# Three more softmax row sums taken off ScalarE in every odd step of an attention block: one to VectorE, two begun on GpSimd and ended on VectorE

## The chip, the cores and the metric

The kernel runs on one core of one Trainium2 chip, as one program. The metric is the device time of one execution in microseconds, taken as the median of several runs. The engines have short names in the views of the profile: PE is TensorE (PEld its weight loads), ACT is ScalarE, DVE is VectorE, POOL is GpSimd, SP is SyncE, which here only issues DMAs.

## What is computed

An attention layer with a condition added to queries and keys, and a residual. `x` is 8 x 512 x 512 in float32, there are 16 heads of 32 columns, and the softmax is over 512 keys.

```python
Q = heads(x @ Wq.T + bq);  K = heads(x @ Wk.T + bk);  V = heads(x @ Wv.T + bv)
cQ = Q + heads(cond @ Wq.T + bq);  cK = K + heads(cond @ Wk.T + bk)
scores = einsum('bhqd,bhkd->bhqk', cQ, cK) / sqrt(32)
x + einsum('bhqk,bhkd->bhqd', softmax(scores), V)      # heads joined again
```

## The kernel before

**Steps and items.** A step `t` is one batch and one group of four heads, so there are 32 steps (8 batches, 4 groups). The loop over `t` from 1 to 28 does each step in four items, `i` = 0 to 3. Item 0 is called `V` in the code: the weighted sum of the step before (`weighted`). The other three make a quarter of the projections for the batch to come, `q`, `k`, `v` in odd steps and `k`, `q`, `v` in even ones, by a Strassen-like scheme with seven products (`four_products` and `three_products`).

**Two ways to the softmax.** Both need the row sums of the exponentials, the softmax's denominators, for 4 query chunks `qc` (128 rows each) and 4 heads `j`: 16 sums a step, called (`qc`, `j`) here and in the code.

- For an even step the scores are made once to find the row maxima and sums (`row_max`, `denominators`), with the exponentials thrown away in PSUM, and a second time transposed (`exponentials`), which gives the operand of the weighted sum.
- For an odd step (`BLOCKED`, `t` = 1, 3 to 27) the exponentials of the first pass are kept in SBUF (the tile `arena`), and DMAs and VectorE's 32 x 32 transposes turn them (`exchange`, `turn_blocks`).

An item looks ahead: at step `t`, items 0 to 2 do maxima and exponentials of chunks 1 to 3 of step `t + 1`, and item 3 does chunk 0 of step `t + 2`. So an odd step's chunk 0 is worked on in item 3 of the odd step before it, and its chunks 1 to 3 in items 0 to 2 of the even step before it.

**Where the sums are made.** `denominators` issues one ScalarE `Exp` for each (`qc`, `j`). With `accum_out` the activation also gives the row sum, and the profile shows it as a second short instruction, ACTIVATION_READ_ACCUMULATOR. For some sums of odd steps from 3 on, `accum_out` is left out and VectorE adds up the exponentials in `arena` (`sum_by_vector`, L729); the table `BY_VECTOR` says which, by the item of the even step that does it:

```python
BY_VECTOR = {1:[(2,0),(2,1)],2:[(3,0),(3,1)]}
```

**Order.** Nothing is scheduled by a tool: each engine runs its instructions in the order in which the code is written, with semaphores between the engines. Names and lines that the steps below use:

- PE: scores L670 (even steps) and L662 (odd steps), transposed scores L784, weighted sum L806, spreading of the sums L843, projections L471.
- ScalarE: `Exp` of the first pass L718, of the second L795, copies of the `v` products out of PSUM L537 and L542.
- VectorE: maxima L626 and L679, reciprocals of the sums L853, the turning of the weighted sum L873, projections' ends L576 and L577, x turned L378, kept exponentials turned L690.
- GpSimd: adds of the projections L559, L561, L563 and L578, of the residual L874 and L875, products for `combine_x` L395 and L396 (in one even step of two), the sums masked L833, a quarter of the exchange's DMAs L701.

PSUM is eight banks; `begin` and `released` give each item its banks in the order in which the items before have let go of them, so a bank that ScalarE or VectorE empties late holds up the matmul that writes it next.

Of the kernel before, what the change touches and what calls it, by code (L numbers as in the profile page):

```python
# [12 lines left out]
ALU = mybir.AluOpType  # L13
AX = mybir.AxisListType
# [3 lines left out]
def kernel(  # L18
# [38 lines left out]
    nc = tc.nc  # L57
    P = 128
# [4 lines left out]
    HG = P // HD  # L63
# [8 lines left out]
    EARLY = 3  # L72
    SINGLY = "qk"
    BY_POOL = (3,)
    BY_VECTOR = {1:[(2,0),(2,1)],2:[(3,0),(3,1)]}
    HELPED = "qk"
    WARM = (48, 4)
    BLOCKED = list(range(1, T - 4, 2))
# [45 lines left out]
    def banks(i, n=1):  # L124

        row = row_of[0] or [at_end[j] for j in TURNS[turn[0]]]
        j = row[i]
        if n == 1:
            return psum[:, j, :]
        k = row[i + 1]  # L130
        return psum[:, j : k + 1 : k - j, :]
# [7 lines left out]
    def begin(w):  # L139
        rows = order[w : w + 4]  # L140
        pairs = [(j, j + 1) for j in rows if j + 1 in rows]
        last = max(pairs, key=lambda p: rows.index(p[0]) + rows.index(p[1]), default=sorted(rows[2:]))
        order[w : w + 4] = sorted(j for j in rows if j not in last) + list(last)
        row_of[0] = list(order)

    def released(*roles):
        order[:] = [row_of[0][i] for i in roles]
# [57 lines left out]
    def add_bias(t):  # L205

        if turned_by_vector(t):
            bias = bvs[:, t % G, :].unsqueeze(1).broadcast_to([P, NB, BL])
        else:
            bias = bvl.broadcast_to([P, S])  # L210
        nc.gpsimd.tensor_tensor(xr[t], xr[t], bias, ALU.add)  # L211
# [12 lines left out]
    def rows_kept(t, half):  # L224

        a = arena[:, half * HG : (half + 1) * HG, :]
        return a.rearrange("p g (c h s) -> p g c h s", c=2, h=HG)
# [104 lines left out]
    def in_place(b):  # L332
# [5 lines left out]
    wT = {  # L338
        n: const.tile([P, NC, D], F32, tag=f"wT{n}", name=f"wT_{n}") for n in ("q", "k", "v")
    }  # L340
# [277 lines left out]
    sums = {}  # L618
# [84 lines left out]
    def denominators(t, qc, w=HG, js=range(HG)):  # L703

        if t >= T - 2:
            return
        for j in js:
            if t in BLOCKED:
                to = rows_kept(t, qc // 2)[:, :, qc % 2, j, :].rearrange(
                    "p g (c e) -> p g c e", e=BL  # L710
                )
            else:
                to = banks(w + j)
            of = banks(w + j)
            if t in BLOCKED:
                of = of.rearrange("p (c g e) -> p g c e", g=HG, e=BL)
            by_vector = t in BLOCKED and t > 1 and any((qc, j) in a for a in BY_VECTOR.values())
            nc.scalar.activation(  # L718
                to,
                of,  # L720
                AF.Exp,
                bias=nmax[t][:, qc, j, :],
                **({} if by_vector else {"accum_out": sums[t][:, qc, j, :]}),
            )

    def sum_by_vector(t, qc, j):

        if t in BLOCKED:
            nc.vector.tensor_reduce(  # L729
                sums[t][:, qc, j, :], rows_kept(t, qc // 2)[:, :, qc % 2, j, :], AX.XY, ALU.add  # L730
            )
# [65 lines left out]
    def times_v(t, kc, pt, chunks=range(NS), half=None):  # L797
        b, g = divmod(t, G)
        at = slice(0, S) if half is None else slice(half * HS, (half + 1) * HS)
        cs = slice(0, NS) if half is None else slice(half * 2, half * 2 + 2)  # L800
        for j in range(HG):
            if t in BLOCKED:
                e = blocked[t][:, :, cs, j, kc * BL : (kc + 1) * BL].rearrange("p a c e -> p c a e")
            else:
                e = es[t, kc, j // 2][:, j % 2, at]
            nc.tensor.matmul(  # L806
                pt[j * HD : (j + 1) * HD, at],
                vs[b % 2][:, kc, (g * HG + j) * HD : (g * HG + j + 1) * HD],
                e,
                start=(kc == chunks[0]),  # L810
                stop=(kc == chunks[-1]),
            )
# [13 lines left out]
    def masked(t):  # L826

        if t in aparts:
            return aparts.pop(t)
        apart = wT["k"][:, t % 2, P : P + HG * NS * NS].rearrange(  # L830
            "p (h c a) -> p h c a", h=HG, c=NS
        )
        nc.gpsimd.tensor_tensor(  # L833
            apart,
            sums[t].rearrange("p c h o -> p h c o").broadcast_to([P, HG, NS, NS]),
            which.unsqueeze(1).unsqueeze(1).broadcast_to([P, HG, NS, NS]),
            ALU.mult,
        )
        return apart

    def spread_sums(apart, pd):
        for h in range(HG):
            nc.tensor.matmul(  # L843
                pd[h * BL : (h + 1) * BL, :NB],
                modulo,
                apart[:, h].rearrange("p c a -> p (c a)"),
                start=True,
                stop=True,
            )

    def reciprocals(t, pd):
        rec = op.tile([P, NB, 1], F32, tag="recs", name=f"recs_{t}")
        nc.vector.reciprocal(rec, pd[:, :NB].unsqueeze(2))  # L853
        return rec

    def weighted(t, pt, pd, between):

        if t:
            add_bias(t)
        apart = masked(t)  # L860
        for half in range(2) if t in BLOCKED else (None,):
            for kc in range(NS):
                times_v(t, kc, pt, half=half)
                if kc == 0 and half != 1:
                    spread_sums(apart, pd)
        rec = reciprocals(t, pd)
        between()
        send(t, pt, rec)

    def send(t, y_, rec):  # L870

        y = op.tile([P, NB, BL], F32, tag="res", name=f"res_{t}", bufs=1)
        nc.vector.transpose(y.rearrange("p f e -> p (f e)"), y_)  # L873
        nc.gpsimd.tensor_tensor(y, y, rec.broadcast_to([P, NB, BL]), ALU.mult)  # L874
        nc.gpsimd.tensor_tensor(xr[t], y, xr[t], ALU.add)  # L875
        if t % 2 or t >= T - 4:
            to_store.append(t)
# [284 lines left out]
        (0, 3): [],  # L1162
    }

    for t in range(1, T - 3):
        b, r = divmod(t, G)
        blocks = t in BLOCKED
        w = 0 if blocks else HG
        items = ["V", "q", "k", "v"] if blocks else ["V", "k", "q", "v"]
        for i, item in enumerate(items):  # L1170
            rows = (t + 1, i + 1) if i < 3 else (t + 2, 0)
            begin(w)
            if not blocks:
                exponentials(t, i)
            late_first = item in ("v" if blocks else "qkv") and t % 2 == 1
            hold = row_max(*rows, late_first, w, not blocks and item in SINGLY)

            def held(i=i, hold=hold):
                hold()
                if i == 2:  # L1180
                    split_max(t + 1)
                    turn_max(t + 1)

            dens = lambda js=range(HG): denominators(*rows, w, js)
            if item in "qkv":
                products(t, item, blocks, held, dens, nothing)
            else:
                held()
                dens()
                if blocks:  # L1190
                    weighted(t - 1, banks(4), banks(5), nothing)
                    released(6, 7, 0, 1, 2, 3, 5, 4)
                else:
                    weighted(t - 1, banks(0), banks(1), nothing)
                    released(2, 3, 1, 4, 5, 6, 7, 0)
            if i == 0 and r % 2 == 0:
                turn_x(t + NC + 2)
                turn_x(t + NC + 3)
            if i == 0 and r == 1:
                combine_x(b + 1, 1, nc.gpsimd)  # L1200
            if i == 1 and r == 0:
                combine_x(b + 1, 0, nc.gpsimd)
            if i == 2:
                aparts[t] = masked(t)
            turn_more(t, i)
            if not blocks:
                for qc, j in BY_VECTOR.get(i, ()):
                    sum_by_vector(t + 1, qc, j)
            for what in ORDERS[t % 2, i]:
                if what == "store":  # L1210
                    store()
                elif what == "residual":
                    if 3 < t + 1 <= T - 4:
                        load_residual(t + 1)
                elif what == "x":
                    load_pairs()
                elif t + 1 in BLOCKED:
                    exchange(t + 1, what)
# [67 lines left out]
    t = T - 3  # L1286
# [25 lines left out]
    t = T - 2  # L1312
# [25 lines left out]
    t = T - 1  # L1338
# [61 lines left out]
    b, g = divmod(t, G)  # L1400
# [55 lines left out]
```

## Time and profile before

| what | value |
|---|---|
| median of 3 runs | 658.34 us (658.25 to 658.65) |
| the profiled execution | 658.21 us, of which its span is 656.1 us |
| granted TensorE clock | 0.999 |
| PE matmuls busy | 649.3 us |
| PE weight loads busy | 305.2 us |
| VectorE busy | 596.4 us |
| ScalarE busy | 538.4 us |
| GpSimd busy | 356.5 us |

Busy time is the time in which at least one instruction of the engine ran. Two steps, an odd and an even one, take 38.9 us together and repeat from about 83 us to 590 us. The readings below are from the pair whose even step begins at 316.70 us (items at 316.70, 322.54, 327.31 and 332.22 us).

### The profile page before, as it was taken

The numbers are of one execution on the slowest core, as the hardware profiler recorded it, in microseconds if no ns is written. First come the engines' busy times: TensorE is split into PE (matmuls) and PEld (weight loads), VectorE is DVE, ScalarE is ACT, GpSimd is POOL, SyncE is SP. The second block draws the span as 40 slices with busy tenths as digits, with TensorE's granted clock in tenths as the row PEclk, the third lists the DMA queues.
The fourth block names the chain that finished last, engine by engine and source line by source line (L and its number), as shares of the span: only waits on it lengthen the run. The fifth ranks groups of instructions, "written<-read, shape, count | busy, mean of one in ns | idle before, by whom it ended". The sixth has DMA issues, their size and how long they took to land.

```text
span 656.1 us, 23961 instructions
## 1 busy us (share of the span) xinstructions
PE 649.3 (99%) x9568; PEld 305.2 (47%) x9568; DVE 596.4 (91%) x868; ACT 538.4 (82%) x1341; POOL 356.5 (54%) x474
## 2 busy tenths in 40 slices
PE   9999999999999999999999999999999999999997
PEld 7444454544445454454444444454554544445432
DVE  4898999999899999999999999999989998996886
ACT  2579798888888888888989979788897988889664
POOL 5642654657536565476645765465754656545440
PEclk9999999999999999999999999999999999999999
DMA  9728648395675938658484765939567592940222
GB/s 206 142 47 209 124 109 208 72 216 126 156 170 117 214 76 213 150 130 195 94 215 99 188 157 130 204 80 221 115 164 168 113 213 47 219 108 6 53 33 33
DMA packets 140819, 90.92 MB, mean 139 GB/s; under 512 B 117436, under 2 KB 126308, under 8 KB 140708
## 3 DMA queue, kind: packets, MB, share of 16 engines
q1 hardware_dynamic: 133252, 73.91, 50.1%
q0 software_dynamic: 5568, 14.95, 9.4%
q8 instruction: 75, 1.23, 0.8%
q10 hardware_dynamic: 1888, 0.52, 0.3%
q14 instruction: 36, 0.29, 0.2%
HBM read 20.27 MB, written 8.39 MB: 44 GB/s over the span
## 4 chain that ended last, share of the span: by engine, by line
PE 94%; POOL 3%; DVE 1%; DMA 1%; issue 1%; ACT 0%; DVEq 0%; POOLq 0%
PE psum L471 43%; PE psum L806 18%; PE psum L670 10%; PE psum L662 9%; PE psum L784 8%; PE psum L781 3%; PE psum L412 1%; PE psum L1262 1%; DMA early<-in_L_cond_Wk_dram 1%; PE psum L1375 0%; POOL early L248 0%; PE psum L843 0%; POOL early L290 0%; ACT psum L718 0%; POOL wc_q L363 0%
## 5 line engine op out<-in xcount | busy, mean ns | idle before, releaser
L626 DVE TENSOR_REDUCE nmax<-psum 128x1 f32<-128x512 f32 x326 | 205.0, 681 | 17.4 <-PE psum L670 13.9
L718 ACT ACTIVATE psum<-psum,nmax 128x512 f32<-128x512 f32 x256 | 169.3, 666 | 46.2 <-DVE nmax L626 34.0
L795 ACT ACTIVATE arena<-psum 128x512 f32<-128x512 f32 x264 | 136.3, 602 | 31.5 <-PE psum L784 24.1
L718 ACT ACTIVATE arena<-psum,nmax 128x512 f32<-128x512 f32 x224 | 148.1, 710 | 5.7 <-issue 4.3
L690 DVE STREAM_TRANSPOSE blocks<-blocks 128x1024 f32<-128x1024 f32 x112 | 132.2, 1219 | 0.0
L679 DVE TENSOR_REDUCE nmax<-psum 128x2 f32<-128x1024 f32 x87 | 105.4, 1212 | 1.1 <-PE psum L670 1.1
L874 POOL TENSOR_TENSOR res<-res,recs 128x512 f32<-128x512 f32 x30 | 31.5, 1050 | 115.2 <-DVE res L873 115.2
L670 PE MATMUL psum<-kT,qT 32*128 32x512 f32 x576 | 85.3, 600 | 0.0
L806 PE MATMUL psum<-arena,v 128*32 128x512 f32 x576 | 68.5, 597 | 0.0
L784 PE MATMUL psum<-qT,kT 32*128 32x512 f32 x528 | 67.9, 587 | 0.0
L701 POOL DMA_DIRECT2D blocks<-arena x112 | 56.1, 507 | 17.7 <-PE psum L784 8.8
L662 PE MATMUL psum<-kT,qT 32*64 32x512 f32 x896 | 62.5, 613 | 0.0
L670 PEld LDWEIGHTS psum<-kT,qT 32*128 32x128 f32 x576 | 38.5, 182 | 30.5 <-issue 10.6
L718 ACT ACTIVATION_READ_ACCUMULATOR psum<-psum,nmax 128x1 f32 x256 | 52.6, 206 | 0.0
L806 PE MATMUL psum<-blocks,v 128*32 128x256 f32 x896 | 52.1, 381 | 0.0
L875 POOL TENSOR_TENSOR xr<-res,xr 128x512 f32<-128x512 f32 x30 | 38.4, 1281 | 2.4
L718 ACT ACTIVATION_READ_ACCUMULATOR arena<-psum,nmax 128x1 f32 x172 | 38.7, 225 | 0.0
L211 POOL TENSOR_TENSOR xr<-xr,wT_q 128x512 f32<-128x512 f32 x30 | 38.5, 1284 | 0.3
L806 PEld LDWEIGHTS psum<-blocks,v 128*32 128x32 f32 x896 | 26.4, 110 | 25.0 <-ACT arena L795 10.6
L873 DVE STREAM_TRANSPOSE res<-psum 128x512 f32<-128x512 f32 x28 | 20.1, 717 | 19.1 <-issue 15.7
L471 PE MATMUL psum<-wT_v,xT 128*32 128x256 f32 x512 | 34.2, 382 | 0.0
L559 POOL TENSOR_TENSOR v<-v 128x512 f32<-128x512 f32 x14 | 17.9, 1278 | 29.4 <-ACT v L542 29.4
(195 smaller groups left out, 1070.3 us busy)
## 6 DMA issues: line engine op xcount, KB each, us to landing
blocks<-arena SPq DMA_DIRECT2D x336, 128.0 KB, 4.2
blocks<-arena POOLq DMA_DIRECT2D x112, 128.0 KB, 4.3
xr<-in_x_dram SPq DMA_DIRECT2D x60, 128.0 KB, 3.0
x<-in_x_dram SPq DMA_DIRECT2D x56, 128.0 KB, 2.8
out_dram<-xr SPq DMA_DIRECT2D x56, 128.0 KB, 2.5
w_q<-in_L_cond_Wq_dram SPq DMA_DIRECT2D x4, 256.0 KB
w_k<-in_L_cond_Wk_dram SPq DMA_DIRECT2D x4, 256.0 KB, 7.4
w_v<-in_L_cond_Wv_dram SPq DMA_DIRECT2D x4, 256.0 KB
```

The costliest lines, as they stand in the source:

```text
L211: nc.gpsimd.tensor_tensor(xr[t], xr[t], bias, ALU.add)
L471: nc.tensor.matmul(pt[r], still[:, r], moving, start=(kc == kcs[0]), stop=(kc == kcs[-1]))
L626: nc.vector.tensor_reduce(nmax[t][:, qc, j : j + 1, 0], pt, AX.X, ALU.max, negate=True)
L662: nc.tensor.matmul(pt[i * n : (i + 1) * n], qkT["q", t][r, qc * P + i * n : qc * P + (i + 1) * n], qkT["k", t][r, :], start=True, stop=True,)
L670: nc.tensor.matmul(pt, qkT["q", t][r, qc * P : (qc + 1) * P], qkT["k", t][r, :], start=True, stop=True,)
L679: nc.vector.tensor_reduce(nmax[t][:, qc, pr * 2 : pr * 2 + 2, 0], pt, AX.X, ALU.max, negate=True)
L690: nc.vector.transpose(e, e)
L701: queue.dma_start(to.rearrange("p c h s -> p (c h s)"), of)
L718: nc.scalar.activation(to, of, AF.Exp, bias=nmax[t][:, qc, j, :], **({} if by_vector else {"accum_out": sums[t][:, qc, j, :]}),)
L784: nc.tensor.matmul(bank[j], qkT["k", t][r, kc * P : (kc + 1) * P], qkT["q", t][r, :], start=False, stop=True,)
L795: nc.scalar.activation(e[:, i, :], bank[pr * 2 + i], AF.Exp)
L806: nc.tensor.matmul(pt[j * HD : (j + 1) * HD, at], vs[b % 2][:, kc, (g * HG + j) * HD : (g * HG + j + 1) * HD], e, start=(kc == chunks[0]), ...
```

## The change

Three more sums of each odd step lose their `accum_out`, for the odd steps 3 to 27 (13 of them):

- (0, 0) is added up by VectorE alone, in item 0 of the even step, between the reciprocals and the turning of the weighted sum.
- (0, 1) is added up in part by GpSimd: three adds of 128 x 128 elements fold four blocks into one, in an unused corner of the tile `wT_k`, behind its activation in item 3 of the odd step before. VectorE ends it with a reduce over 128 elements a row, just ahead of (0, 0).
- (2, 2) likewise: GpSimd's three adds stand at the end of item 1 of the even step, VectorE's short reduce in item 2, ahead of the two sums that it makes there already.

```diff
-    BY_VECTOR = {1:[(2,0),(2,1)],2:[(3,0),(3,1)]}
+    BY_VECTOR = {0: [(0, 0)], 1: [(2, 0), (2, 1)], 2: [(3, 0), (3, 1)]}
+    IN_PART = {0: (0, 1), 1: (2, 2)}
+    PART_AT = {0: 0, 1: 2}
...
-            by_vector = t in BLOCKED and t > 1 and any((qc, j) in a for a in BY_VECTOR.values())
+            by_vector = t in BLOCKED and t > 1 and (
+                any((qc, j) in a for a in BY_VECTOR.values()) or (qc, j) in IN_PART.values()
+            )
...
+            if by_vector and (qc, j) == IN_PART.get(0):
+                sum_in_part(t, qc, j)
+
+    part = wT["k"][:, 0:2, P + P // 2 : 2 * P]
+
+    def sum_in_part(t, qc, j):
+        if t in BLOCKED:
+            e = rows_kept(t, qc // 2)[:, :, qc % 2, j, :].rearrange("p g (i s) -> p g i s", i=2)
+            for g in range(1, HG):
+                nc.gpsimd.tensor_tensor(part, part if g > 1 else e[:, 0], e[:, g], ALU.add)
+
+    def sum_part(t, qc, j):
+        if t in BLOCKED:
+            nc.vector.tensor_reduce(sums[t][:, qc, j, :], part, AX.XY, ALU.add)
...
+    def more_sums(t, i):
+        for k, at in PART_AT.items():
+            if at == i:
+                sum_part(t + 1, *IN_PART[k])
+        for qc, j in BY_VECTOR.get(i, ()):
+            sum_by_vector(t + 1, qc, j)
...
-                    weighted(t - 1, banks(0), banks(1), nothing)
+                    weighted(t - 1, banks(0), banks(1), lambda: more_sums(t, 0))
...
-                for qc, j in BY_VECTOR.get(i, ()):
-                    sum_by_vector(t + 1, qc, j)
+                if i:
+                    more_sums(t, i)
+                if i in IN_PART and i:
+                    sum_in_part(t + 1, *IN_PART[i])
```

The order of PE's and SyncE's instructions stays. On VectorE, in item 0 of an even step, this stands before (from the second maxima of the item to the turning of x):

```order
L626 TENSOR_REDUCE nmax_1538<-psum 128x1 x2
L679 TENSOR_REDUCE nmax_1538<-psum 128x2
L853 RECIPROCAL recs_1660<-psum 128x16
L873 STREAM_TRANSPOSE res_1662<-psum 128x512
L378 STREAM_TRANSPOSE xT_1174<-x_1471 128x512 x2
```

and this now, with the line numbers of the changed kernel (L744 is `sum_part`, L749 `sum_by_vector`, L893 the turning of the weighted sum, L873 now the reciprocals):

```order
L628 TENSOR_REDUCE nmax_1547<-psum 128x1 x2
L681 TENSOR_REDUCE nmax_1547<-psum 128x2
L873 RECIPROCAL recs_1672<-psum 128x16
L744 TENSOR_REDUCE sums_1548<-wT_k 128x1
L749 TENSOR_REDUCE sums_1548<-arena 128x1
L893 STREAM_TRANSPOSE res_1676<-psum 128x512
```

Two reduces have come between the reciprocals and the turning. On ScalarE, with the semaphores that each instruction waits for, item 3 of an odd step has before, from the first `Exp` of chunk 0 to the second pass of the next step (`sums` among the outputs marks the accumulators):

```order
L718 ACTIVATE arena,sums_1052<-psum,nmax_1051 128x4x128 [waits DMAHW3_49,DMAHW4_49,DMAHW0_49,DMAHW5_49,DMASW1_49,DMAHW6_49,DMASW0_49,DMAHW7_49,DVE_49,Pool_49]
L718 ACTIVATE arena,sums_1052<-psum,nmax_1051 128x4x128 [waits DVE_49] x2
L537 COPY v_156<-psum 128x2x256 [waits PE_49,Activation_49]
L718 ACTIVATE arena,sums_1052<-psum,nmax_1051 128x4x128 [waits DVE_49]
L542 COPY v_156<-psum 128x2x256 [waits PE_49,Activation_49]
L795 ACTIVATE arena<-psum 128x512 [waits PE_49] x4
```

and now:

```order
L722 ACTIVATE arena<-psum,nmax_1051 128x4x128 [waits DMAHW4_49,DMAHW3_49,DMAHW5_49,DMAHW0_49,DMAHW6_49,DMASW1_49,DMAHW7_49,DMASW0_49,DVE_49]
L722 ACTIVATE arena<-psum,nmax_1051 128x4x128 [waits DVE_49]
L722 ACTIVATE arena,sums_1052<-psum,nmax_1051 128x4x128 [waits DVE_49,Pool_49]
L539 COPY v_156<-psum 128x2x256 [waits PE_49,Activation_49]
L722 ACTIVATE arena,sums_1052<-psum,nmax_1051 128x4x128 [waits DVE_49]
L544 COPY v_156<-psum 128x2x256 [waits PE_49,Activation_49]
```

The first two exponentials have no accumulator any more, and the wait for GpSimd has moved from the first to the third. In item 3 of the even step, where the second pass writes over the part of `arena` that GpSimd has read, the first `Exp` waited for four DMA semaphores, PE and ScalarE before, and waits for GpSimd too now. On GpSimd, from item 0 of an even step to its item 2, this stands now (L739 `sum_in_part`, L580 the adds that end the `k` and `q` projections, L853 the masked sums, L703 the exchange):

```order
L703 DMA blocks_2187<-arena 32x1024 x4
L580 TENSOR_TENSOR kT_2006<-wT_k,kT_2006 128x256
L739 TENSOR_TENSOR wT_k<-arena 128x2x64
L739 TENSOR_TENSOR wT_k<-wT_k,arena 128x2x64 x2
L580 TENSOR_TENSOR qT_1936<-wT_q,qT_1936 128x256
L853 TENSOR_TENSOR wT_k<-sums_1841,which 128x64
L703 DMA blocks_2187<-arena 32x1024 x4
```

The rows of L739 are new, the others stood in this order before. The other three adds stand in item 3 of an odd step, between the masked sums and the first add of the `v` projection (L559 before).

## The prediction

> **What bounds the kernel now.** I read the page first (busy times and the chain that ended last), then PE's timeline over one pair of steps, and then asked of each place where PE loses time what it waits for.
>
> ```profile
> PE 649.3 (99%) x9568; PEld 305.2 (47%) x9568; DVE 596.4 (91%) x868; ACT 538.4 (82%) x1341; POOL 356.5 (54%) x474
> PE 94%; POOL 3%; DVE 1%; DMA 1%; issue 1%; ACT 0%; DVEq 0%; POOLq 0%
> ```
>
> TensorE runs throughout, and the chain is TensorE for 94%. Work taken off ScalarE can therefore only pay where PE's stream is stretched by a late bank of PSUM. Equal groups of matmuls show where that is. These are the eight matmuls of L670 in items 0 to 3 of one even step, and in item 0 of the next one (start, length of the group):
>
> ```profile
> 317.79 1.16 PE L670 MATMUL psum<-kT,qT 32*128 32x512 f32 x8
> 323.63 1.03 PE L670 MATMUL psum<-kT,qT 32*128 32x512 f32 x8
> 328.40 1.16 PE L670 MATMUL psum<-kT,qT 32*128 32x512 f32 x8
> 333.31 1.03 PE L670 MATMUL psum<-kT,qT 32*128 32x512 f32 x8
> ...
> 356.67 1.16 PE L670 MATMUL psum<-kT,qT 32*128 32x512 f32 x8
> ```
>
> The same work takes 1.03 us in items 1 and 3 and 1.16 in items 0 and 2, so 0.13 us is lost twice in each pair of steps, at the same places in the next pair. The weight loads show how:
>
> ```profile
> 317.37 0.19 PEld L670 LDWEIGHTS psum<-kT,qT 32*128 32x128 f32 x3 [0.24 <-ACT arena L718]
> 317.79 0.33 PEld L670 LDWEIGHTS psum<-kT,qT 32*128 32x128 f32 x5 [0.24 <-issue]
> ...
> 327.98 0.19 PEld L670 LDWEIGHTS psum<-kT,qT 32*128 32x128 f32 x2 [0.24 <-DVE kT L576]
> 328.40 0.32 PEld L670 LDWEIGHTS psum<-kT,qT 32*128 32x128 f32 x6 [0.24 <-issue]
> ```
>
> In item 0 three loads are made ahead and the fourth comes only at 317.79, in item 2 two are made ahead and the third comes after 328.40: a head's bank isn't free yet.
>
> ScalarE holds the bank in item 0. Its rows in item 3 of the odd step before (start, length):
>
> ```profile
> 314.03 0.69 ACT L718 ACTIVATE arena<-psum,nmax 128x512 f32<-128x512 f32 x1 [0.36 <-issue]
> ...
> 314.71 0.68 ACT L718 ACTIVATE arena<-psum,nmax 128x512 f32<-128x512 f32 x1
> ...
> 315.37 0.69 ACT L718 ACTIVATE arena<-psum,nmax 128x512 f32<-128x512 f32 x1
> ...
> 317.18 0.60 ACT L542 COPY v<-psum 128x512 f32<-128x512 f32 x1
> 317.99 2.06 ACT L795 ACTIVATE arena<-psum 128x512 f32<-128x512 f32 x4 [0.20 <-PE psum L784]
> ```
>
> From 314.03 on ScalarE doesn't pause until L542 ends at 317.18 + 0.60 = 317.78, where the fourth load goes. In item 2 it is the last `Exp` of item 1, whose accumulator reading ends at 328.12 + 0.26 = 328.38:
>
> ```profile
> 325.75 1.87 ACT L718 ACTIVATE arena<-psum,nmax 128x512 f32<-128x512 f32 x3
> 327.46 0.25 ACT L718 ACTIVATION_READ_ACCUMULATOR arena<-psum,nmax 128x1 f32 x1
> 327.55 0.73 ACT L718 ACTIVATE arena<-psum,nmax 128x512 f32<-128x512 f32 x1
> 328.12 0.26 ACT L718 ACTIVATION_READ_ACCUMULATOR arena<-psum,nmax 128x1 f32 x1
> ```
>
> So the three sums that the change takes off ScalarE stand right ahead of the two places where PE loses time.
>
> **What an accumulator costs.** A reading is listed with 0.25 us, but overlaps what follows: the next `Exp` starts 327.55 - 327.46 = 0.09 us behind it. Agreeing, `Exp`s with accumulators follow each other at 0.66 to 0.68, those without at (1.87 - 0.69) / 2 = 0.59. I take 0.09 for each.
>
> **Gain at item 0.** (0, 0) and (0, 1) are the first two of ScalarE's run from 314.03, so two readings, 0.18 us, go. VectorE, which delivers the maxima, caps that:
>
> ```profile
> L626 DVE TENSOR_REDUCE nmax<-psum 128x1 f32<-128x512 f32 x326 | 205.0, 681 | 17.4 <-PE psum L670 13.9 <-PE psum L662 2.8
> ```
>
> (a group of the page), and in the timeline
>
> ```profile
> 313.26 2.48 DVE L626 TENSOR_REDUCE nmax<-psum 128x1 f32<-128x512 f32 x4
> 321.38 0.24 DVE L853 RECIPROCAL recs<-psum 128x16 f32<-128x16 f32 x1
> 322.73 0.72 DVE L873 STREAM_TRANSPOSE res<-psum 128x512 f32<-128x512 f32 x1 [1.12 <-issue]
> ...
> 327.87 0.42 DVE L577 TENSOR_TENSOR wT_k<-psum,wT_k 128x256 f32<-128x256 f32 x1
> ...
> 332.79 1.27 DVE L729 TENSOR_REDUCE sums<-arena 128x1 f32<-128x512 f32 x2
> 334.36 1.29 DVE L626 TENSOR_REDUCE nmax<-psum 128x1 f32<-128x512 f32 x2 [0.30 <-PE psum L670]
> ```
>
> Four maxima of 0.68 in 2.48 follow each other at 0.60. The first ends at 313.94, and its `Exp` starts 0.09 later, at 314.03. The third ends at 315.14, so the third `Exp` starts no earlier than about 315.23, against 315.37. All behind it comes 0.14 earlier: L542 ends at 317.64, the fourth load goes at about 317.65, and nearly all of the 0.13 is won.
>
> What is late next? The spreading of the sums, whose bank is that of the second `Exp` of L795. Four of those in 2.06, the last of them 0.60, follow each other at 0.49, so the second ends at 317.99 + 0.49 + 0.60 = 319.08. L795 starts on matmuls ahead of the stall and doesn't move.
>
> ```profile
> 319.19 0.29 PEld L843 LDWEIGHTS psum<-wT_k,modulo 128*32 128x32 f32 x8
> ...
> 336.99 0.23 PEld L662 LDWEIGHTS psum<-kT,qT 32*64 32x64 f32 x16 [0.41 <-issue]
> ```
>
> These loads start 0.11 behind that release. PE, 0.13 ahead of before, may give back between 0 and 0.11 here. No row says which; I take 0.04, below the middle, since these are the smallest matmuls of the stream (16 columns), and so 0.09 won, of bounds 0.02 to 0.13.
>
> **Gain at item 2.** Without the reading of (2, 2) the last `Exp` of item 1 ends 0.09 earlier, at 328.29. VectorE's L577, which empties the next bank, ends then too (327.87 + 0.42 = 328.29), so no more than 0.09 of the 0.13 comes from this. What is late next is item 0 of the odd step: its L662 loads go at 336.99, and the `Exp` that frees one of their banks is done 0.04 before:
>
> ```profile
> 333.55 2.06 ACT L795 ACTIVATE arena<-psum 128x512 f32<-128x512 f32 x4 [0.40 <-ACT arena L718]
> ...
> 336.71 0.24 ACT L718 ACTIVATION_READ_ACCUMULATOR psum<-psum,nmax 128x1 f32 x1
> ```
>
> ScalarE's run to there starts at 333.55 on PE's L784 and moves with PE, but its first `Exp` now waits for one semaphore more, GpSimd's. That was fulfilled long ago; going through the list costs time all the same. No row prices one wait. Bounds are 0 and 0.09, the start of the `Exp` at 314.03 behind a whole list. I take 0.03, as one of several, which leaves 0.06, with bounds 0 and 0.13 (should L577 move up too).
>
> **What VectorE gets.** A sum over 512 elements took 0.676; two in 1.27 follow each other at 0.59. A reduce over 128 has no row. It lies between the 0.24 for 16 elements (L853) and the 0.42 for 256 (below); I take 0.28, and 0.20 from start to start.
>
> ```profile
> L729 DVE TENSOR_REDUCE sums<-arena 128x1 f32<-128x512 f32 x52 | 33.0, 676 | 0.0
> L577 DVE TENSOR_TENSOR wT_k<-psum,wT_k 128x256 f32<-128x256 f32 x14 | 5.8, 416 | 0.1
> ```
>
> Item 0 then has 0.20 + 0.59 = 0.79 more in front of L873, which idles 1.12 ahead of it until PE's weighted sum ends: hidden, 0.33 to spare, 0.2 when PE comes earlier. If that cover were gone, each 0.1 us would cost PE nearly as much, 1.3 us in all, since item 1's matmuls at 323.63 write the bank that L873 leaves at 323.45. The Trainium skill, VectorE: DVE Perf Modes (The DRAIN you can't avoid), says that the next operation doesn't start until the pipe is empty. Our two sums overlap by 0.08; by that page the two new reduces would take 0.96, still under 1.12, and the sum would be the same with less to spare. Item 2 gets 0.20, under the 0.30 of idling at 334.36.
>
> **What GpSimd gets.** Six adds of 128 x 128 a pair.
>
> ```profile
> L833 POOL TENSOR_TENSOR wT_k<-sums,which 128x64 f32<-128x64 f32 x30 | 8.9, 295 | 0.0
> L561 POOL TENSOR_TENSOR qT<-wT_q,qT 128x256 f32<-128x256 f32 x14 | 10.3, 732 | 1.1
> ```
>
> (groups by line), and in the timeline
>
> ```profile
> 317.86 1.28 POOL L559 TENSOR_TENSOR v<-v 128x512 f32<-128x512 f32 x1 [2.13 <-ACT v L542]
> ...
> 369.09 1.28 POOL L396 TENSOR_TENSOR xc<-xc,xT 128x512 f32<-128x512 f32 x1
> 371.82 0.72 POOL L578 TENSOR_TENSOR qT<-wT_q,qT 128x256 f32<-128x256 f32 x1 [1.45 <-DVE wT_q L577]
> ```
>
> Between 0.295 for 64 elements and 0.732 for 256 lies 0.44; with 0.08 between dependent ones, three take 1.6. In item 3 of the odd step they fill the 2.13 of idling ahead of L559. In item 1 of the even step they lie ahead of L578; where `combine_x` runs too (6 pairs) they end at 370.37 + 1.6 = 371.97 against an idling that ends at 371.82. There L578, the masked sums and the DMAs behind them come 0.15 later, and VectorE's short reduce waits some 0.3, so that VectorE is 0.2 late at item 3. The maxima late there feed `Exp`s behind the one at 336.71, whose banks PE asks for only behind the group of L662 at 336.99, so I cost it at nothing; at the worst it takes 6 x 0.2 = 1.2 us.
>
> **The sum.** 0.09 + 0.06 = 0.15 us a pair, in 13 pairs 1.95 us. The profiled execution took 658.21, of which 2.1 us lie around its span of 656.1; 658.21 - 1.95 = 656.26, and with the 0.13 by which the median of 658.34 lies above it, 656.4 us. A measurement of this kernel tells about 0.2%, 1.3 us, from no change.
>
> **The rivals.**
> - *The next gates take it back* (spreading of the sums and L662, both at their low bounds, or GpSimd's lateness in six pairs). For it: the margins of 0.11 and 0.04 us. Against it: small loads, and ScalarE moving along with PE. (0.02 + 0.02) x 13 = 0.5 us, 657.8. Chance 0.20.
> - *Both stalls go whole*: 0.26 x 13 = 3.4, 655.0. For it: VectorE has room ahead of L873. Against it: L577 ends at the same 328.29. Chance 0.13.
> - *VectorE is the bound, and the change loads it.* The place is L873 in item 0: it decides once the two reduces take over about 1.2 us, 1.5 times what I count. For it: VectorE is busy 91%. Against it: the idling of 1.12 and 0.30. If all that is added lay on the path, 0.20 + 0.59 + 0.20 = 0.99 us a pair is 12.9 us: 671.2; with a third of it, 662.5. Chance 0.12. The Trainium skill, Perfetto Trace Analysis (Identifying the Most-Contended Engine), would rank it so: occupancy is a fair measure for Vector but matmul busy is not for Tensor, for which weight load busy is to be taken (here 47%). Against that stand the equal 1.03 us of L670 and idling VectorE.
> - *The change doesn't do what it says*: the first odd step keeps its accumulators (14 odd steps, 13 changed), which is counted; the order of instructions shows the other 13 changed, so I give this none.
>
> **How the numbers follow.** The forecast (655.2 to 657.0) has 0.55. Faster by over 0.2% (below 657.0) is the forecast and the whole gain: 0.68. Within 0.2% is the first rival, 0.20; slower the third, 0.12. The range runs from the whole gain, 655.0 less 0.1, to no gain at all with the spread of the runs, 658.5, and leaves out the slower case.
>
> **What would show it.** Right: groups of L670 at 1.03 to 1.08 in items 0 and 2 of the pairs from the second on; L542 ending 0.14 earlier against item 0's L784; L873 still released by PE; idling of VectorE ahead of it down to about 0.3. Wrong: L873 starting behind a reduce with PE's weighted sum long over, L843 or L662 groups longer than before, or L670 still at 1.16.

## The result, and the profile after

The changed kernel takes 656.55 us (median of 12 runs, 655.99 to 658.07), the kernel before on the same chip 658.39 us (12 runs, 657.84 to 659.38): a ratio of 0.9974, with an interval of 0.9965 to 0.9982. The profiled execution took 655.99 us, its span is 654.2 us. Its page (busy times, and the chain that ended last):

```profile
PE 647.4 (99%) x9568; PEld 308.9 (47%) x9568; DVE 608.7 (93%) x907; ACT 536.3 (82%) x1302; POOL 390.8 (60%) x552
PE 96%; DVE 2%; DMA 1%; POOL 0%; issue 0%; DVEq 0%
```

VectorE works 12 us more, GpSimd 34 us more, ScalarE 2 us less, and the chain is still PE's. PE's timeline, the score matmuls of items 0 to 3 of the same even step as before (start, length), and then the first scores of the odd step behind it:

```profile
316.46 1.03 PE L672 MATMUL psum<-kT,qT 32*128 32x512 f32 x8
...
322.20 1.03 PE L672 MATMUL psum<-kT,qT 32*128 32x512 f32 x8
...
326.98 1.06 PE L672 MATMUL psum<-kT,qT 32*128 32x512 f32 x8
...
331.79 1.11 PE L672 MATMUL psum<-kT,qT 32*128 32x512 f32 x8
...
335.56 1.11 PE L664 MATMUL psum<-kT,qT 32*64 32x512 f32 x16
```

Item 0 has lost its whole stall (1.16 to 1.03), item 2 most of it (1.16 to 1.06). Item 3 has a new one: 1.03 before, 1.11 now. Setting PE's stream beside that of before, group by group, a pair of steps wins 0.132 us at item 0 and gives back 0.027 at the spreading of the sums right behind it; it wins 0.092 at item 2 and gives back 0.088 at item 3. So 0.11 us is left of 0.22. ScalarE's rows say who holds item 3 up:

```profile
330.90 0.73 ACT L722 ACTIVATE arena<-psum,nmax 128x512 f32<-128x512 f32 x1
331.47 0.26 ACT L722 ACTIVATION_READ_ACCUMULATOR arena<-psum,nmax 128x1 f32 x1
332.11 0.60 ACT L815 ACTIVATE arena<-psum 128x512 f32<-128x512 f32 x1 [0.38 <-DMA blocks<-arena]
```

The reading of (3, 3) ends at 331.73, and the fourth head's weights of item 3 are loaded from 331.775 on, 0.01 ahead of the group's first matmul. The kernel before, in the same place (weight loads, ScalarE):

```profile
332.88 0.62 PEld L670 LDWEIGHTS psum<-kT,qT 32*128 32x128 f32 x8 [0.23 <-issue]
```

```profile
332.90 0.26 ACT L718 ACTIVATION_READ_ACCUMULATOR arena<-psum,nmax 128x1 f32 x1
```

There that reading ended at 333.16, and the fourth of these loads went at 333.20, still 0.10 ahead of the first matmul at 333.31.

VectorE, item 0 of that step (timeline), and two groups by line (busy time, mean ns | idle time ahead):

```profile
320.05 0.24 DVE L873 RECIPROCAL recs<-psum 128x16 f32<-128x16 f32 x1
320.21 0.23 DVE L744 TENSOR_REDUCE sums<-wT_k 128x1 f32<-128x128 f32 x1
320.36 0.67 DVE L749 TENSOR_REDUCE sums<-arena 128x1 f32<-128x512 f32 x1
321.24 0.72 DVE L893 STREAM_TRANSPOSE res<-psum 128x512 f32<-128x512 f32 x1 [0.21 <-PE psum L826]
```

```profile
L739 POOL TENSOR_TENSOR wT_k<-wT_k,arena 128x128 f32<-128x128 f32 x52 | 23.8, 458 | 4.1
L744 DVE TENSOR_REDUCE sums<-wT_k 128x1 f32<-128x128 f32 x26 | 6.6, 254 | 0.9 <-POOL wT_k L739 0.9
```

The turning still waits for PE, 0.21 where it waited 1.12.

### The profile page after: what moved, and what is told of

The parts are those of the page before. It is cut to its first block, busy times and chain, and to the rows that moved or that the text cites. A ratio compares the mean times of both kernels' runs of the same rounds, so it can differ in the third digit from the quotient of the medians.

```text
span 654.2 us, 24014 instructions
## 1 busy us (share of the span) xinstructions
PE 647.4 (99%) x9568; PEld 308.9 (47%) x9568; DVE 608.7 (93%) x907; ACT 536.3 (82%) x1302; POOL 390.8 (60%) x552
## 4 chain that ended last, share of the span: by engine, by line
PE 96%; DVE 2%; DMA 1%; POOL 0%; issue 0%; DVEq 0%
PE psum L473 44%; PE psum L826 18%; PE psum L672 10%; PE psum L664 9%; PE psum L804 9%; PE psum L801 3%; PE psum L414 2%; DMA early<-in_L_cond_Wk_dram 1%; PE psum L1292 0%; PE psum L1405 0%; PE psum L933 0%; DVE nmax L1310 0%; DVE nmax L681 0%; POOL early L250 0%; PE psum L863 0%; POOL early L292 0%
## 5 line engine op out<-in xcount | busy, mean ns | idle before, releaser
L815 ACT ACTIVATE arena<-psum 128x512 f32<-128x512 f32 x264 | 136.3, 602 | 32.7 <-PE psum L804 25.6
L722 ACT ACTIVATE arena<-psum,nmax 128x512 f32<-128x512 f32 x224 | 145.7, 710 | 5.0 <-DVE nmax L628 3.7
L672 PE MATMUL psum<-kT,qT 32*128 32x512 f32 x576 | 83.8, 598 | 0.0
L703 POOL DMA_DIRECT2D blocks<-arena x112 | 56.1, 507 | 17.7 <-PE psum L804 8.8
L664 PE MATMUL psum<-kT,qT 32*64 32x512 f32 x896 | 62.4, 613 | 0.0
L749 DVE TENSOR_REDUCE sums<-arena 128x1 f32<-128x512 f32 x65 | 41.7, 675 | 0.0
L826 PEld LDWEIGHTS psum<-blocks,v 128*32 128x32 f32 x896 | 30.6, 110 | 21.1 <-ACT arena L815 10.6
L473 PE MATMUL psum<-wc_v,xc 128*32 128x256 f32 x512 | 33.5, 379 | 0.0
L826 PEld LDWEIGHTS psum<-arena,v 128*32 128x32 f32 x576 | 14.7, 110 | 38.0 <-issue 19.9
```

Source lines behind the costliest of these rows:

```text
L473: nc.tensor.matmul(pt[r], still[:, r], moving, start=(kc == kcs[0]), stop=(kc == kcs[-1]))
L664: nc.tensor.matmul(pt[i * n : (i + 1) * n], qkT["q", t][r, qc * P + i * n : qc * P + (i + 1) * n], qkT["k", t][r, :], start=True, stop=True,)
L672: nc.tensor.matmul(pt, qkT["q", t][r, qc * P : (qc + 1) * P], qkT["k", t][r, :], start=True, stop=True,)
L703: queue.dma_start(to.rearrange("p c h s -> p (c h s)"), of)
L722: nc.scalar.activation(to, of, AF.Exp, bias=nmax[t][:, qc, j, :], **({} if by_vector else {"accum_out": sums[t][:, qc, j, :]}),)
L749: nc.vector.tensor_reduce(sums[t][:, qc, j, :], rows_kept(t, qc // 2)[:, :, qc % 2, j, :], AX.XY, ALU.add)
```

## The experiments

A whole run scatters by 1 us and more, in part because what lies ahead of the pairs differs from execution to execution: the first pair counted here begins anywhere from 95.38 to 96.91 us in the thirteen profiles, and in the two profiles of the changed kernel at 95.38 and 95.95. The pairs themselves repeat to 0.02 us in most of a run, and the same kernel's medians to 0.01 from chip to chip. So each kernel is read twice: by its runs, and by the length of a pair, the median of 12 in a row, taken from one even step's `q` projection to the next one's.

| kernel | sums moved | pair, us | less than before | runs, us | ratio to the kernel before |
|---|---|---|---|---|---|
| before | – | 38.87 | – | 658.15 to 658.41 | 1 |
| changed | (0,0) (0,1) (2,2) | 38.76 | 0.11 | 656.55 | 0.9974 (0.9965 to 0.9982) |
| 1 | (0,0) (0,1) | 38.84 | 0.03 | 657.80 | 0.9996 (0.9988 to 1.0005) |
| 2 | (2,2) | 38.86 | 0.01 | 657.79 | 0.9994 (0.9985 to 1.0003) |
| 3 | changed and (3,2) | 38.75 | 0.12 | 656.33 | 0.9973 (0.9963 to 0.9983) |
| 4 | (0,0) (0,1) (3,2) | 38.84 | 0.03 | 657.48 | 0.9988 (0.9979 to 0.9997) |
| 5 | as 1, wait put early | 38.76 | 0.11 | 656.41 | 0.9974 (0.9965 to 0.9983) |
| 6 | changed, wait put early | 38.76 | 0.11 | 656.14 | 0.9970 (0.9959 to 0.9982) |
| 7 | as 3, wait put early | 38.67 | 0.20 | 655.49 | 0.9964 (0.9951 to 0.9976) |
| 8 | changed, (0,1) by VectorE alone | 38.77 | 0.10 | 656.42 | 0.9977 (0.9966 to 0.9987) |
| 9 | changed, again | 38.76 | 0.11 | 656.30 | 0.9970 (0.9959 to 0.9982) |
| 10 | 7, again | 38.68 | 0.19 | 655.97 | 0.9961 (0.9949 to 0.9974) |
| 11 | as 3, (0,1) by VectorE alone | 38.69 | 0.19 | 655.12 | 0.9951 (0.9938 to 0.9963) |

1 to 4 ran on one chip, 5 to 8 on a second, 9 to 11 on a third. The theory at the start was that item 2's gain is lost at item 3, and that all of what remains is item 0's. The rivals: item 2's gain stays (A), or VectorE's added short reduce causes item 3's loss (B).

**1. Without (2, 2).**

```diff
-    IN_PART = {0: (0, 1), 1: (2, 2)}
-    PART_AT = {0: 0, 1: 2}
+    IN_PART = {0: (0, 1)}
+    PART_AT = {0: 0}
```

> The changed kernel with the sum (2,2) left on ScalarE's Exp; (0,0) and (0,1) leave it as changed. Theory (what item 2 gains is lost again at item 3, because ScalarE's Exp of (3,3) does not move and the fourth head's weight load waits for it): no slower than the changed kernel, 656.6 us within 0.4, score matmul groups of items 0 to 3 at 1.03, 1.03, 1.16, 1.03. Rival A (item 2's 0.09 us of a pair stays, item 3's longer group has another cause outside this edit): 0.09 x 13 = 1.2 us less gain, 657.3 to 657.8. Rival B (item 3's longer group comes from VectorE's extra short reduce in item 2): also 656.6, but told apart by the next two kernels.

It was slower than expected by 1.2 us: 657.80, and 0.03 us a pair instead of 0.11. The time is the one that rival A gave, but not for its reason: the groups came out as foreseen, item 3's at 1.03 again, so its stall does belong to the edit. The loss turned up where nobody had looked, in the next step's first scores. Timelines of this kernel (PE, its weight loads, ScalarE):

```profile
333.76 1.03 PE L672 MATMUL psum<-kT,qT 32*128 32x512 f32 x8
...
337.46 1.18 PE L664 MATMUL psum<-kT,qT 32*64 32x512 f32 x16
```

```profile
337.46 0.29 PEld L664 LDWEIGHTS psum<-kT,qT 32*64 32x64 f32 x16 [0.41 <-issue]
```

```profile
334.08 2.07 ACT L815 ACTIVATE arena<-psum 128x512 f32<-128x512 f32 x4 [0.48 <-DMA blocks<-arena]
...
337.24 0.24 ACT L722 ACTIVATION_READ_ACCUMULATOR psum<-psum,nmax 128x1 f32 x1
```

The L664 group takes 1.18 instead of 1.11, and its sixteen weight loads 0.29 instead of 0.23: behind the second of them there is a gap of 0.05, until ScalarE's second reading is over (337.24 + 0.24 = 337.48). ScalarE is late because L815 begins 334.08 - 333.76 = 0.32 us behind item 3's scores; in the kernel before that is 333.55 - 333.31 = 0.24. The rows of ScalarE's sequencer in the trace show what lies between. L815 writes over a part of `arena` that GpSimd's additions have read, so it waits for one semaphore more. Before, the last semaphore instruction ahead of it ended at 333.503, when PE's transposed scores were there, and the `Exp` began 0.045 later. Here that one ends at 333.962, one more follows it (334.000 to 334.038), for semaphores that had long been met, and the `Exp` begins at 334.083, 0.121 later. That is 0.076 us more, and the same in ten of the eleven pairs compared. Both kernels have three semaphore instructions there; with seven semaphores instead of six, the one that PE sets has moved from the third of them to the second. (The row of L815 names a block's DMA as what ended the wait; by these rows it was PE.)

So there are two gates behind item 2, and they give a second theory, in numbers per pair. PE can win 0.105 with (0, 0) and (0, 1), and 0.092 with (2, 2). *Gate A*, item 3's fourth weight load, waits for (3, 3): ScalarE's run to there starts ahead of item 2's stall, so it moves only by what item 0 has won, and by 0.09 more if (3, 2) has no accumulator either. *Gate B*, the third weight load of the odd step, moves by all that PE has won up to item 3, less 0.076 where L815 waits for GpSimd. The smaller gate decides. For this kernel B gives 0.105 - 0.076 = 0.03, as measured; for the changed one A gives 0.105 and B 0.12, hence 0.105. This theory was made with the results of 1 to 4 at hand; 5 to 11 test it.

**2. Only (2, 2).**

```diff
-    BY_VECTOR = {0: [(0, 0)], 1: [(2, 0), (2, 1)], 2: [(3, 0), (3, 1)]}
-    IN_PART = {0: (0, 1), 1: (2, 2)}
-    PART_AT = {0: 0, 1: 2}
+    BY_VECTOR = {1: [(2, 0), (2, 1)], 2: [(3, 0), (3, 1)]}
+    IN_PART = {1: (2, 2)}
+    PART_AT = {1: 2}
```

> The kernel before with only (2,2) moved (added up in part by GpSimd, ended by VectorE). Theory: no gain, 658.4 us within 0.4, groups of items 0 to 3 at 1.16, 1.03, 1.06, 1.11. Rival A (item 2's gain stays): 1.2 us faster, 657.2.

By the pair, as the theory at the start said: 0.01 us, with item 2 at 1.06 and item 3 at 1.11 (PE's timeline):

```profile
288.86 1.06 PE L672 MATMUL psum<-kT,qT 32*128 32x512 f32 x8
...
293.67 1.11 PE L672 MATMUL psum<-kT,qT 32*128 32x512 f32 x8
```

Gate A stays where it was and takes all of it back. Rival A's 657.2 is out by the pair (it needs 38.78); the runs alone, 657.79 in an interval of 0.9985 to 1.0003, only lean that way.

**3. The changed kernel, and (3, 2) too.**

```diff
-    IN_PART = {0: (0, 1), 1: (2, 2)}
+    IN_PART = {0: (0, 1), 1: (2, 2), 3: (3, 2)}
...
-                    weighted(t - 1, banks(4), banks(5), nothing)
+                    ended = (lambda: sum_part(t, *IN_PART[3])) if t > 1 else nothing
+                    weighted(t - 1, banks(4), banks(5), ended)
```

> The changed kernel with one more sum taken off ScalarE: (3,2), added in part by GpSimd at the end of the even step's item 3 and ended by VectorE in the next odd step's item 0. Theory (item 3's stall is ScalarE's run of Exps coming late): (3,3) is ready 0.09 us earlier, the item 3 group goes back to 1.03 and about 0.09 x 13 = 1.2 us are gained on the changed kernel: 655.4 us (655.0 to 655.9). Rival B (VectorE's short reduce causes item 3's stall): no gain, 656.5, and slower by up to 0.2 x 13 = 2.6 us if the short reduce in item 0 of the odd step pushes VectorE's weighted sum past its 0.2 us of idle time.

Item 3's stall goes, which shows that (3, 3) on ScalarE made it, and rules out rival B: VectorE's short reduce in item 2 is still there.

```profile
327.68 1.06 PE L672 MATMUL psum<-kT,qT 32*128 32x512 f32 x8
...
332.49 1.03 PE L672 MATMUL psum<-kT,qT 32*128 32x512 f32 x8
...
336.19 1.18 PE L664 MATMUL psum<-kT,qT 32*64 32x512 f32 x16
```

But of the 0.09 only 0.02 is won: now gate B holds (1.18), at 0.197 - 0.076 = 0.12. The expected 655.4 was missed by 0.9 us.

**4. (3, 2) in the place of (2, 2).** `IN_PART = {0: (0, 1), 3: (3, 2)}`, `PART_AT = {0: 0}`, and the second edit of 3.

> The changed kernel with (2,2) back on ScalarE and (3,2) taken off it in its stead. Theory (the two stalls of items 2 and 3 lie behind one another on ScalarE, so that either sum alone gives nothing): groups 1.03, 1.03, 1.16, 1.03, the time of the changed kernel, 656.6 us within 0.4. Rival A (each sum stands for 0.09 us by itself): with item 3 not stalled in this kernel there is nothing to take, 657.5. Rival B (VectorE's short reduce in item 2 is the cause): 656.6 too.

0.03 us a pair, as kernel 1. ScalarE is done 0.09 earlier ahead of L815 and waits that much longer for it:

```profile
332.92 2.06 ACT L815 ACTIVATE arena<-psum 128x512 f32<-128x512 f32 x4 [0.57 <-DMA blocks<-arena]
```

It idles 0.57 instead of 0.48: what starts L815 isn't ScalarE's own work but the semaphores. The expected 656.6 rested on the first theory, which gate B overturns. Rival A's 657.5 came true in time, but what it supposes, that each sum is worth 0.09 by itself, is out by the pair of kernel 2.

**5. Kernel 1 with the wait put early.** A dependency on the third addition is given to the `Exp` of (1, 1). That stands in item 0 of the even step (not in item 1, as the expectation has it), long before the first L815 of item 3, which then needs no check of its own for it: in the trace it waits for six semaphores again, with PE's in the last semaphore instruction. (Its own lines move L815 to L825.)

```diff
-            nc.scalar.activation(
+            exp = nc.scalar.activation(
...
+            if t in added and (qc, j) == (1, 1):
+                tc.add_manual_dep(
+                    exp.ins,
+                    added[t].ins.name,
+                    mybir.DependencyInfo(mybir.DependencyClass.Sync, mybir.DependencyReason.DATA),
+                    reason="early",
+                )
...
-                nc.gpsimd.tensor_tensor(part, part if g > 1 else e[:, 0], e[:, g], ALU.add)
+                last = nc.gpsimd.tensor_tensor(part, part if g > 1 else e[:, 0], e[:, g], ALU.add)
+            if (qc, j) == IN_PART.get(0):
+                added[t] = last
```

> Only (0,0) and (0,1) moved, as in the first experiment, and ScalarE's wait for GpSimd's additions is put on an Exp in the middle of item 1, where it has long been met and is read ahead behind a running Exp; so ScalarE's first weight Exp of item 3 waits for no more semaphores than in the kernel before. New theory (the added wait makes that Exp start 0.12 us after its release where 0.045 was; ScalarE is 0.076 us later from there on, and the score matmuls of the next step's item 0 wait 0.07 us for it): item 3's weight Exp again 0.04 to 0.05 us after its release, the 0.06 us gap within the first group of score matmuls of the next step gone, 0.106 us a pair gained instead of 0.03, and 0.07 x 13 = 0.9 us less than the first experiment: 656.9 us, about 1.4 less than the kernel before. Rival (the wait has no part in it, PE's groups there depend on something else that the sums of item 0 bring): 657.8 as in the first experiment.

As the second theory said, 0.11 us a pair, and the gap is gone. The runs have 656.41, 0.5 less than expected.

```profile
333.04 1.02 PE L672 MATMUL psum<-kT,qT 32*128 32x512 f32 x8
...
336.72 1.11 PE L664 MATMUL psum<-kT,qT 32*64 32x512 f32 x16
```

```profile
333.28 2.06 ACT L825 ACTIVATE arena<-psum 128x512 f32<-128x512 f32 x4 [0.40 <-ACT arena L722]
```

L825 begins 0.24 behind the scores again, as L795 before, and 0.045 behind the last semaphore instruction. With (2, 2) left on ScalarE this kernel is as fast as the changed one.

**6. The changed kernel with the wait put early** (the edit of 5).

> The changed kernel with the same wait put early. New theory: the time of the changed kernel, 656.5 us (ratio to the kernel before 0.9974 within 0.001), since there item 3's score group loses 0.09 us a pair first, to the Exp of (3,3), and the late weight Exp stands in nobody's way. Rival (the wait costs 0.07 us a pair whatever else): 0.9 us less, 655.6.

38.76 us a pair, as without the early wait: nothing won, since gate A decides there. (The runs alone, 656.14, lie between the expected 656.5 and the rival's 655.6.) It also shows what (2, 2) is worth by itself: 5 and 6 differ by it alone, and their pairs are equal.

**7. The changed kernel, (3, 2) too, the wait put early** (the edits of 3 and 5).

> The changed kernel with (3,2) moved too, as in the third experiment, and the wait put early. New theory: with item 3's stall gone and the wait hidden, nothing gives back what items 0 and 2 gain: 0.106 + 0.097 = 0.20 us a pair against 0.13 in the third experiment, 0.9 us less: 655.4 us, a ratio of 0.9960 (0.9950 to 0.9968) to the kernel before. Rival (the wait has no part in it): 656.3, ratio 0.9973.

Both gates open: 38.67 us, 0.20 a pair, as the sum 0.105 + 0.092 says, and 655.49 us.

```profile
327.65 1.06 PE L672 MATMUL psum<-kT,qT 32*128 32x512 f32 x8
...
332.46 1.03 PE L672 MATMUL psum<-kT,qT 32*128 32x512 f32 x8
...
336.14 1.11 PE L664 MATMUL psum<-kT,qT 32*64 32x512 f32 x16
```

**8. (0, 1) by VectorE alone.** `BY_VECTOR` gets `0: [(0, 0), (0, 1)]`, `IN_PART = {1: (2, 2)}`, `PART_AT = {1: 2}`.

> The changed kernel with (0,1) summed by VectorE alone: two full reductions of 0.6 us between item 0's reciprocals and the turning of its weighted sum, where VectorE had 1.12 us idle before, and no additions by GpSimd there. The prediction's step on cover (0.33 us was left of that idle time; 0.4 us more work, start to start, makes the turning late by about 0.1): the turning waits for nothing any more and comes late, PE loses 0.05 to 0.15 us a pair after item 0, so 657.2 to 658.5 us. Rival (VectorE has room, since others wait for its turning later than the trace suggests): 656.5, the time of the changed kernel, and as the weight Exp of item 3 has no additional wait here, nothing is lost there either.

The turning does come late, but PE hardly notices, as the rival had it: 656.42, 0.10 us a pair, 0.01 less than in the changed kernel. VectorE's timeline:

```profile
320.50 0.24 DVE L873 RECIPROCAL recs<-psum 128x16 f32<-128x16 f32 x1
320.67 1.21 DVE L749 TENSOR_REDUCE sums<-arena 128x1 f32<-128x512 f32 x2
321.80 0.70 DVE L893 STREAM_TRANSPOSE res<-psum 128x512 f32<-128x512 f32 x1
```

It begins 1.30 behind the reciprocals instead of 1.19, and waits for nothing. GpSimd isn't needed for (0, 1), then.

**9. The changed kernel again, 10. kernel 7 again, 11. kernel 3 with (0, 1) by VectorE alone,** on one chip. The expectation of 11 puts the three reduces into one item; the two full ones stand in item 0 of the even step, the short one in item 0 of the odd step.

> The changed kernel as it is, on the same chip as the two below, so that all three share the runs of the kernel before: a ratio of 0.9974 within 0.001, and 38.77 us from one odd step's start to the next.

> The kernel of the seventh experiment ((3,2) moved too, the wait put early) beside the changed kernel: 38.67 us a pair against 38.77, so 0.1 x 13 = 1.3 us less than the changed kernel, a ratio near 0.996 to the kernel before. Rival (the pair's gain is lost outside the pairs): the changed kernel's time.

> Another way to the same: (0,1) summed by VectorE alone, so that no additions of GpSimd stand before item 3's weight Exp, and (2,2) and (3,2) in part by GpSimd. Theory of the added wait: no added wait here, so both gains stay, less the 0.01 us a pair that the late turning cost: 38.68 us a pair, the time of the seventh experiment's kernel within 0.3 us. Rival (the early wait brought something else): 38.75 us as in the third experiment, 0.9 us more. What could also stand in the way: item 0 of the odd step then holds two full and one short reduction on VectorE, more than its idle time there; each 0.1 us by which PE waits for it costs 1.3 us.

Both ways past gate B give 38.68 and 38.69 us a pair, where 3, with the wait, had 38.75. By its runs, though, kernel 10 is only 0.3 us faster than 9, where 1.3 was expected. In the two profiles the twelve pairs are 0.97 us shorter, but what lies behind them is 0.50 longer, so its rival, that the gain is lost outside the pairs, isn't ruled out for the whole time. Kernel 11 has the best time of all, 655.12 us, 3.3 less than the kernel before and 1.2 less than the changed one beside it, with VectorE busier than in any other:

```profile
PE 646.3 (99%) x9568; PEld 307.6 (47%) x9568; DVE 613.7 (94%) x920; ACT 535.4 (82%) x1289; POOL 390.3 (60%) x552
```

Between 10 and 11 the pairs differ by 0.01 only; the 0.85 us between their medians, where at most 0.3 was expected, lies outside them (in the profiles 0.8 behind the last pair), and whether that is the kernel's or chance isn't settled.

## Why the prediction was right or wrong

- **The bound** was read rightly: PE's equal groups at unequal lengths. Experiment after experiment follows those lengths to 0.01 us a pair. The Trainium skill, Perfetto Trace Analysis (Identifying the Most-Contended Engine), takes the engine with the highest occupancy, and judges TensorE by its weight loads and its share of peak arithmetic. By busy times, 91% against 47% of weight loads, that would be VectorE (the share of peak isn't worked out here); the trace says otherwise, since kernel 11 gives VectorE 17 us more and is the fastest.
- **An accumulator's price**, 0.09, was right: without (2, 2) the last `Exp` of item 1 and its reading end 0.09 earlier in ScalarE's run, and PE's item 2 gains 0.092.
- **Item 0**: forecast 0.09 (0.13 less 0.04 for the spreading of the sums), measured 0.132 - 0.027 = 0.105. The first rival's place is real, but costs a quarter of what it could.
- **Item 2** is the step that failed. The 0.09 was right. "What is late next is item 0 of the odd step" was not: item 3's own scores come first, and they wait for (3, 3), which ScalarE ended at 333.16 against scores at 333.31 in the kernel before; the loss shows that this left no room. They took 0.088 back, so the term of 0.06 measured 0.00. The bound that the prediction put beside it, VectorE's L577, didn't hold: its counterpart, L579, ends at 326.66 in the changed kernel, 0.2 ahead of ScalarE's reading, and the 0.03 that is left of the stall is still ScalarE's (the weight loads go on at 326.91, 0.05 behind its reading). The wait named as the cost was there, at 0.076 instead of 0.03; in the changed kernel gate A covers it, in kernels 1, 3 and 4 it is what decides. The Trainium skill, Perfetto Trace Analysis (Identifying Dependency Chains), says that instructions which wait on several engines may get semaphore instructions put ahead of them; the trace agrees, and adds that one behind the last release costs 0.076.
- **The sum**: 0.15 us a pair was forecast, 0.11 measured, 1.4 us in 13 pairs instead of 1.95. That 656.4 came so close to 656.55 is therefore partly luck. The medians differ by 1.84 (by 2.1 in kernel 9's runs), and not all of it comes from the pairs: of the 1.9 us between the two profiled spans, 12 pairs account for 1.30, a single late start of ScalarE's L795 at 178 us, in the kernel before alone of these two, for 0.27 (the trace doesn't show what it waited for), and the rest lies ahead of and behind the pairs.
- **VectorE's cover** was right in size (0.21 left of 1.12, forecast 0.2 to 0.33; the short reduce 0.254 against 0.28). What it would cost without cover was wrong: kernel 8 has none and loses 0.01, not 0.1. The prediction's own rows offer a reason: item 1's matmuls at 323.63 against a bank left at 323.45 is a margin of 0.18, and the turning came 0.11 late. The Trainium skill, VectorE: DVE Perf Modes (The DRAIN you can't avoid), has the next operation wait until the pipe is empty, and the prediction took the end of the listed time for that. Here L749 starts 0.15 behind L744, which is listed with 0.23, so listed times do overlap; when the pipe is empty no row shows.
- **GpSimd**: additions of 0.458 against 0.44 forecast; three take 1.53, where the prediction had 1.6 (its own terms give 1.48). VectorE's wait for them in six pairs is 0.9 us in all, half of what was forecast, and the lengths of the pairs don't show it.

## What to carry to other kernels

Ahead of an edit that shortens one engine's run, list every later point in the loop at which the bound engine waits for that engine, with the margin of each: a gain passes only as far as the tightest of them, and two edits that are worth nothing alone can be worth 0.1 us together. A dependency on another engine can cost something even when it was met long ago (0.076 us here), if it puts a check behind the last release; hand it to an earlier instruction that runs behind others. Where a loop repeats, its length in the profile resolves far more than the time of whole runs: 0.01 us in 38.9 here, where runs scattered by 1 us. What happens outside the loop it doesn't show.

## What the runs showed of the hardware

- ScalarE went through L815's semaphores in the order of the list, one or two at a time: L815 began 0.121 us behind its release with one semaphore instruction behind the one that was released last, 0.045 with none. The two checks ahead of the last release cost nothing that shows.
- One late weight load moved all that followed: in kernel 1 the sixteen loads of L664 stopped for 0.05 behind the second, and the last of them and the group's end came 0.06 later behind the first than in the kernel before.
- Taking work off an engine that idles 18% of the time paid only in the places where its short run ended at a gate: the readings of (0, 0) and (0, 1) gave 0.105 us a pair, that of (2, 2) nothing until (3, 2) left too.
